# Feed-forward products as four column groups of the array, in a kernel of two attentions and a feed-forward block

## The chip, the cores and the metric

The kernel runs on one core of a Trainium2 chip. The metric is the device time of one execution in microseconds (us). The engines of the core are named as in the profile: PE is TensorE (matmuls), PEld its weight loads, DVE is VectorE, ACT is ScalarE, POOL is GpSimd, and SP issues most transfers.

## What is computed

The input x has shape (2, 256, 128, 128): batch, time, band, channel, all in fp32. Three blocks follow each other, each with a layer norm ahead of it and a residual sum behind it:

```
x = x + mha_over_time(ln(x))      # 4 heads of 32, causal over 256 times, for each band
x = x + mha_over_bands(ln(x))     # 4 heads of 32, |i - j| <= 16 over 128 bands, for each time
h = gelu(ln(x) @ w1.T + b1)       # 128 -> 512
x = x + (h @ w2.T + b2)           # 512 -> 128
```

The matrices of the attentions are 128 x 128 for query, key, value and output. A token has 128 channels, and there are 65536 tokens.

## The kernel before

The work is cut into groups of 512 tokens: 128 groups of attention over time (class OverTime), 128 over bands (OverBands), and 128 of feed-forward (FeedForward). First all time groups run. Then 16 runs follow; each has 8 band groups and after them 8 feed-forward groups over the same tokens. Changes from bands to feed-forward occur 16 times, back to bands 15 times.

The method run (from L1031) writes out the order of everything by hand, step by step. A step n holds pieces of several neighbouring groups: the scores or first hidden products of group n, the products that consume the softmax or the gelu of group n - 1 (weigh), the output projection of n - 2, projections of queries, keys and values of n + 1 or n + 2, and normalization of groups further on. Each engine runs its instructions in exactly this order, since every call goes through InOrder (L851), which pins it. That is why nearly all lines of the profile read L861: groups of instructions are told apart by the tile that they write.

The tiles of TensorE are these. xnT is the normalized input, channels on the partitions, 512 tokens. qp, kp (L568) and vp (L587) are the projections; sp the scores; rp the sums of the exponentials, by a product with ones; op the weighted values; yp (L627) the output projection. In feed-forward, hp (L808) is a hidden product, four a group, each with 512 tokens as moving columns; zp (L836) is the second product: for each of four blocks of 128 tokens it accumulates four products over the hidden index j, so sixteen products of 128 moving columns a group. All these tiles take turns in the 8 banks of PSUM. A product with fp32 operands appears in the trace as two MATMUL records and two weight loads.

An attention has a head in each band of 32 columns or rows of the array. Its scores use 32 rows of the array for a head (32*128 in the profile); rp and op use 32 columns for a head (128*32). Full products show as 128*128. For the projections, the helper product (L643) has both forms. With by_columns it issues four matmuls, each with 32 columns of the weights and 32 partitions of the output, all with the same moving operand; without, it issues one. run sets by_columns at L1058, once for each step: true where group n - 1 is an attention. The projections of steps behind a feed-forward group are therefore issued in full form: 66 qp and kp, 132 vp (33 groups) and 64 yp (16 groups), the few groups at the start of the program among them. hp and zp do not use the helper and are always in full form.

At a change from bands to feed-forward the step called turn first issues all four hp of the first feed-forward group, then rp, op and yp of the band groups that are still open. The next step has two hp, the zp of the first group, two hp, and the last yp of the bands. At a change back, the projections and scores of the first band groups stand between the last hp and zp. DVE normalizes, corrects the reciprocal of rp (writing rp, u, oT), adds residuals, and masks one head in four; ACT does exp, gelu and the copies out of PSUM; POOL masks and adds.

Of the kernel before, what the change touches and what calls it, by code (L numbers as in the profile page):

```python
# [19 lines left out]
P = 128  # L20
# [404 lines left out]
class Group:  # L425
# [117 lines left out]
    def weigh(self):  # L543
        pass
# [14 lines left out]
class Attention(Group):  # L559
# [8 lines left out]
    def queries_keys(self):  # L568
        path = self.path
        wf = path.k.wf[self.which]  # L570
        self.qp = path.bank([P, NT * P], "qp", self.place.get("qp", path.held.pop("qp", None)))
        product(path, self.qp, wf[:, 0:P], self.xnT)

        self.kp = path.bank([P, NT * P], "kp", self.place.get("kp"))
        product(path, self.kp, wf[:, P : 2 * P], self.xnT)
# [11 lines left out]
    def values(self):  # L587
        path = self.path
        wv = path.k.wf[self.which][:, 2 * P : 3 * P]
        self.vp = path.bank([P, NT, P], "vp", self.place.get("vp"))  # L590
        for i in range(NT):
            product(path, self.vp[:, i], self.xnT[:, i * P : (i + 1) * P], wv)
# [46 lines left out]
def rows_of(h):  # L639
    return slice(h * D, (h + 1) * D)  # L640


def product(path, out, weights, x):  # L643

    if not path.by_columns:
        path.tensor.matmul(out, weights, x, start=True, stop=True)
        return
    for c in range(P // D):
        path.tensor.matmul(out[rows_of(c)], weights[:, rows_of(c)], x, start=True, stop=True)


class OverTime(Attention):
# [75 lines left out]
def time_scores(old, new):  # L728


    if new is not None:
        new.first_tiles()
    if old is not None:
        old.second_tiles()
    for h, second, s in (
        (0, 1, 0), (1, 0, 0), (2, 0, 0), (3, 1, 0), (0, 1, 1), (3, 1, 1), (0, 0, 0), (3, 0, 0),
        (1, 0, 1), (2, 0, 1), (0, 0, 1), (3, 0, 1), (1, 1, 0), (2, 1, 0), (1, 1, 1), (2, 1, 1),
    ):
        if second and old is not None:
            old.second_scores(h, s)  # L740
        if not second and new is not None:
            new.first_scores(h, s)
# [57 lines left out]
class FeedForward(Group):  # L800
# [7 lines left out]
    def hidden(self, js):  # L808
        path = self.path
        for j in js:  # L810
            self.hp[j] = path.bank([P, NT * P], "hp")
            path.tensor.matmul(self.hp[j], path.k.w1f[:, j * P : (j + 1) * P], self.xnT, start=True, stop=True)

    def gelus(self, js):
        path = self.path
# [20 lines left out]
    def weigh(self):  # L836
        path, NI = self.path, self.path.k.NI
        self.zp = path.bank([P, NT, P], "zp")
        for i in range(NT):
            for j in range(NI):  # L840
                path.tensor.matmul(
                    self.zp[:, i], self.hT[:, j, i * P : (i + 1) * P], path.k.w2T[:, j, :],
                    start=(j == 0), stop=(j == NI - 1),
                )

# [20 lines left out]
class BoundedPath:  # L866
# [164 lines left out]
    def run(self, x, out):  # L1031
        groups = list(self.groups(x, out))

        def do(n, *names):
            if 0 <= n < len(groups):
                for name in names:
                    getattr(groups[n], name)()

        def at(n, kind):
            return 0 <= n < len(groups) and isinstance(groups[n], kind)  # L1040

        def do_at(n, kind, *names):
            if at(n, kind):
                do(n, *names)
# [8 lines left out]
        for n in range(-12, len(groups) + 2):  # L1053
            feeds = [at(n - 2 + i, FeedForward) for i in range(5)]
            bands = [at(n - 2 + i, OverBands) for i in range(5)]
            turn = feeds[2] and bands[1]
            old, new = (groups[i] if at(i, OverTime) else None for i in (n, n + 1))
            self.by_columns = at(n - 1, Attention)  # L1058
            if bands[2] and feeds[1]:
                self.scalar.preload_act_table_set(EXP_SET)  # L1060
            do_at(n + 4, FeedForward, "root")
            do(n, "first_half", "first_function", "first_mask")
            if old is not None or new is not None:
                time_scores(old, new)
                b = self.banks
                Attention.place = dict(rp=b["b0"], op=b["b3"], yp=b["a1"], qp=b["a2"], kp=b["b1"], vp=b["b2"])
            else:
                Attention.place = {}
            if old is not None:
                old.second_weights(old.late)  # L1070
            if new is not None:
                new.first_weights(new.early)
            if old is not None:
                old.second_weights(old.early)
                old.mask_second()
                old.add(0)
            if turn:
                do(n, "second_half", "second_function")
            do_at(n + 3, OverTime, "fetch")
            do_at(n + 2, (OverBands, FeedForward), "fetch")  # L1080

            for i in (2 * n + 12, 2 * n + 13) if n < -2 else (n + 10,) if n < 2 else ():
                if i >= NT:
                    do(i, "load")
            if n < -8 or n >= 0:
                do(n + 12, "load")
            if n >= 0:
                do_at(n + 5, OverTime, "statistics")
                for i in due[n]:
                    do(i, "statistics")  # L1090
            do_at(n + 3, (OverBands, FeedForward), "normalize", "turn")
            do_at(n + 4, OverTime, "normalize", "turn")
            if n < 0:
                do(n + 5, "statistics")
            do_at(n + 5, FeedForward, "statistics")
            if n == -4:
                self.fold_rest()
                self.warm()
            do(n - 1, "weigh")
            do(n - 1, "invert_exactly" if turn else "invert")  # L1100
            if new is not None:
                new.first_weights(new.late)
                new.mask_first()
            if old is not None:
                old.add(1)
            if bands[2] or turn or old is not None:
                do(n - 2, "output", "finish")
            do(n - 1, "divide")
            if not turn:
                do(n, "second_half", "second_function")  # L1110
            if n in run0:
                do(n, "bias")
            if not bands[2] and old is None:
                do_at(n, FeedForward, "bias")
                do_at(n + A, OverBands, "bias")
                if at(n - 1, FeedForward) and at(n - 2, OverBands):
                    do_at(n + A - 1, OverBands, "statistics", "root")
                if not turn:
                    do_at(n + A, OverBands, "statistics", "root")
            do_at(n + 2, OverTime, "queries_keys", "take_query", "take_key")  # L1120
            do_at(n + 1, OverBands, "queries_keys", "take_query", "take_key")
            do_at(n + 5, OverTime, "root_by_scalar", "refine")
            for i in due[n]:
                do(i, "root_by_scalar", "refine")
            do_at(n, OverTime, "bias")
            if not bands[2] and not turn and old is None:
                do(n - 2, "output", "finish")
            do_at(n + 2, OverTime, "values", "take_values")
            do_at(n + 1, OverBands, "values", "take_values")
            if old is not None or new is not None:  # L1130

                b = self.banks
                self.banks = dict(
                    a1=b["a1"], a2=b["a2"], b0=b["a0"], b3=b["a3"], a0=b["b0"], a3=b["b1"], b1=b["b3"], b2=b["b2"]
                )
# [69 lines left out]
```

## Time and profile before

| | |
|---|---|
| time, median of 3 runs | 2729.12 us (2726.89 to 2729.46) |
| span of the profiled run | 2727.3 us |
| granted clock of TensorE | 0.998 of full |
| busy DVE, ACT, POOL | 2280.3, 1846.0, 1861.1 us |
| records of MATMUL, of weight loads | 43538 each |
| the chain that ended last: PE, DVE | 83%, 13% |

The profile was taken on one execution. A line of groups gives the line, the engine, the operation, the tile written and the tiles read, the part of the array as rows*columns, the shape, the number of records, and behind the bar the busy time in us and the mean of one record in ns; behind the second bar is the idle time of the engine ahead of them. A line of the timeline gives the start in us, the length in us, and then the same names; x32 means that 32 records were merged. The ends of matmuls are modelled, and records of TensorE may overlap. In the chain of waits, the products zp and hp hold 17% and 14% of the span.

### The profile page before, as it was taken

To read this page: it belongs to the slowest core of one execution; us is meant where nothing else is said; L and a number is where in the kernel's file an instruction comes from. 1 tells how busy PE (TensorE), PEld (TensorE's weight loads), DVE (VectorE), ACT (ScalarE), POOL (GpSimd) and SP (SyncE) were. 2 spreads that over 40 slices of the span, in tenths; PEclk is the share of its full clock that TensorE was granted. 3 is DMA by queue.
4 is the path that set the end of the run, shared out by engine and by line. 5 is a ranking of instruction groups with operands and counts; after the bars stand their busy time and mean duration, and the time that the engine had idled before them with its cause. 6 is when DMAs were issued, how large, how long until landed. Compare 5 with 4: busy or idle time off the path is not lost.

```text
span 2727.3 us, 105790 instructions
## 1 busy us (share of the span) xinstructions
PE 2697.7 (99%) x43538; PEld 1884.5 (69%) x43538; DVE 2280.3 (84%) x6708; ACT 1846.0 (68%) x3620; POOL 1861.1 (68%) x2169
## 2 busy tenths in 40 slices
PE   7999999999999999999999999999999999999998
PEld 5666667767667667676676776766766767767666
DVE  7999999999999987968869779688697796886874
ACT  6888888888888874655745646556556466465563
POOL 3887888888788776666656666666576665665762
PEclk9999999999999999999999999999999999999999
DMA  5555555555555544444444444454453444534533
GB/s 147 146 149 142 146 151 141 152 147 142 145 153 143 136 108 120 116 117 126 111 119 127 106 120 118 116 129 106 121 130 102 122 120 110 135 108 115 132 91 79
DMA packets 471310, 343.84 MB, mean 126 GB/s; under 512 B 43296, under 2 KB 405152, under 8 KB 470816
## 3 DMA queue, kind: packets, MB, share of 16 engines
q1 hardware_dynamic: 469568, 335.92, 47.5%
q8 instruction: 344, 5.64, 0.9%
q10 hardware_dynamic: 1248, 1.05, 0.2%
q14 instruction: 150, 1.23, 0.2%
HBM read 169.03 MB, written 167.77 MB: 123 GB/s over the span
## 4 chain that ended last, share of the span: by engine, by line
PE 83%; DVE 13%; DMA 2%; issue 1%; SPq 0%; ACT 0%; DVEq 0%; ACTq 0%
PE zp L861 17%; PE hp L861 14%; PE sp L861 10%; PE op L861 8%; PE rp L861 7%; PE vp L861 7%; PE qp L861 6%; PE kp L861 6%; PE yp L861 6%; DVE xh L861 3%; DVE stats L861 2%; DVE z L861 2%; DVE u L861 2%; DVE rp L861 1%; DMA xnT<-turned 1%; DVE x L861 1%
## 5 line engine op out<-in xcount | busy, mean ns | idle before, releaser
L861 ACT ACTIVATE hT<-hp,b 128x512 f32<-128x512 f32 x512 | 347.8, 687 | 544.0 <-PE hp L861 533.1
L861 POOL TENSOR_SCALAR_AFFINE_SELECT pf<-pf 128x512 f32<-128x512 f32 x768 | 476.9, 635 | 268.8 <-ACT pf L861 242.5
L861 DVE TENSOR_SCALAR xh<-x,mv,rstd 128x160 f32<-128x160 f32 x1536 | 597.3, 432 | 14.2
L861 PEld LDWEIGHTS zp<-w2T_sb,hT 128*128 128x128 f32 x4096 | 476.3, 192 | 56.2 <-issue 54.0
L861 PE MATMUL zp<-w2T_sb,hT 128*128 128x128 f32 x4096 | 479.8, 275 | 0.1
L861 PE MATMUL hp<-xnT,w1f 128*128 128x512 f32 x1024 | 469.2, 596 | 0.0
L861 ACT ACTIVATE p<-sp 128x512 f32<-128x512 f32 (+1 forms) x1024 | 417.1, 501 | 17.3 <-PE sp L861 4.8
L861 POOL TENSOR_SCALAR_AFFINE_SELECT p<-p 128x1024 f32<-128x1024 f32 x256 | 280.1, 1094 | 191.8 <-ACT p L861 191.8
L861 PE MATMUL sp<-qT,kT 32*128 32x128 f32 (+1 forms) x8192 | 362.4, 310 | 3.2 <-DVE oT L861 1.9
L861 PEld LDWEIGHTS sp<-qT,kT 32*128 32x128 f32 x8192 | 310.1, 185 | 54.5 <-ACT kT L861 44.4
L861 PEld LDWEIGHTS vp<-wf,xnT 128*32 128x32 f32 (+1 forms) x7400 | 237.5, 113 | 153.3 <-issue 137.0
L861 POOL TENSOR_TENSOR p<-p,p 128x512 f32<-128x512 f32 x256 | 328.5, 1283 | 10.7
L861 DVE BATCH_NORM_STATS2 stats<-x 128x6 f32<-128x128 f32 x1536 | 327.0, 276 | 0.8 <-DMA x<-in_x 0.8
L861 ACT ACTIVATE pf<-sp 128x512 f32<-128x512 f32 x512 | 264.7, 603 | 60.8 <-PE sp L861 60.1
L861 PEld LDWEIGHTS hp<-xnT,w1f 128*128 128x128 f32 x1024 | 182.1, 190 | 174.7 <-issue 109.3
L861 DVE TENSOR_TENSOR res<-zp,res 128x512 f32<-128x512 f32 x128 | 87.5, 684 | 237.0 <-PE zp L861 237.0
L861 DVE STREAM_TRANSPOSE z<-xh 128x512 f32<-128x512 f32 x384 | 273.3, 712 | 13.2
L861 POOL TENSOR_SCALAR rstd<-mv 128x4 f32<-128x4 f32 x248 | 56.3, 227 | 319.6 <-DVE mv L861 318.5
L861 PE MATMUL vp<-wf,xnT 128*32 128x128 f32 (+1 forms) x7400 | 272.0, 273 | 0.0
L861 PE MATMUL yp<-wn,oT 128*32 128x128 f32 (+1 forms) x7808 | 271.2, 273 | 0.0
L861 POOL TENSOR_TENSOR rstd<-rstd,mhalf 128x4 f32<-128x4 f32 x248 | 256.6, 1035 | 20.7
L861 ACT ACTIVATE qT<-qp,bq 128x512 f32<-128x512 f32 x256 | 176.0, 687 | 137.5 <-PE qp L861 137.5
(92 smaller groups left out, 4215.9 us busy)
## 6 DMA issues: line engine op xcount, KB each, us to landing
turned<-z SPq DMA_DIRECT2D x1536, 64.0 KB, 1.9
xnT<-turned SPq DMA_DIRECT2D x384, 256.0 KB, 3.0
x<-in_x SPq DMA_DIRECT2D x128, 256.0 KB, 4.2
x<-res SPq DMA_DIRECT2D x256, 128.0 KB, 2.4
x<-x SPq DMA_DIRECT2D x128, 256.0 KB, 4.1
out<-res SPq DMA_DIRECT2D x256, 128.0 KB, 2.5
w1T_sb<-in_w1T ACTq DMA_DIRECT2D x1, 256.0 KB, 7.1
w2T_sb<-in_w2T ACTq DMA_DIRECT2D x1, 256.0 KB, 8.5
```

The source lines that it names most:

```text
L861: return self.tc.keep_in_program_order(emit(*args, **kwargs))
```

## The change

All products with full weights are issued in one form of the array. The helper loses its full form and takes the flags of accumulation; hp and zp are issued through it; the switch by_columns goes, so that the projections at the changes are in columns too. Each product becomes four matmuls of 32 weight columns that write 32 partitions each. The purpose is that the array stays in column groups from one product to the next, and leaves that form only for the scores. What is computed, the banks, and the order of products stay as they are.

```
-def product(path, out, weights, x):
-
-    if not path.by_columns:
-        path.tensor.matmul(out, weights, x, start=True, stop=True)
-        return
+def product(path, out, weights, x, start=True, stop=True):
     for c in range(P // D):
-        path.tensor.matmul(out[rows_of(c)], weights[:, rows_of(c)], x, start=True, stop=True)
+        path.tensor.matmul(out[rows_of(c)], weights[:, rows_of(c)], x, start=start, stop=stop)
...
-            path.tensor.matmul(self.hp[j], path.k.w1f[:, j * P : (j + 1) * P], self.xnT, start=True, stop=True)
+            product(path, self.hp[j], path.k.w1f[:, j * P : (j + 1) * P], self.xnT)
...
-                path.tensor.matmul(
-                    self.zp[:, i], self.hT[:, j, i * P : (i + 1) * P], path.k.w2T[:, j, :],
+                product(
+                    path, self.zp[:, i], self.hT[:, j, i * P : (i + 1) * P], path.k.w2T[:, j, :],
                     start=(j == 0), stop=(j == NI - 1),
                 )
...
-            self.by_columns = at(n - 1, Attention)
```

## The prediction

> **What bounds the kernel now.** I read the busy shares first, then the groups of TensorE, the windows of single steps, the waits of TensorE, and last its timeline at the steps that the diff touches. The shares say that one engine is full from end to end:
>
> ```profile
> PE 2697.7 (99%) x43538; PEld 1884.5 (69%) x43538; DVE 2280.3 (84%) x6708; ACT 1846.0 (68%) x3620; POOL 1861.1 (68%) x2169
> ```
>
> Of 2727.3 us TensorE (PE) lacks 30. Whole steps taken by windows say who is second. The first is one feed-forward step, the second one band step, from a product's start to the same product of the next step:
>
> ```profile
> 2043.17:2050.18 7.01, 7.01 (x42) 5.10 (x41) 3.92 (x15) 2.75 (x5) 3.74 (x6) 1.00 0.48 136
> 2088.59:2095.02 6.43, 6.43 (x160) 4.32 (x155) 6.29 (x19) 5.04 (x10) 4.95 (x9) 1.00 0.41 106
> ```
>
> The columns are length, then busy PE, PEld (weight loads), DVE, ACT, POOL. In the feed-forward step PE is full and the next, DVE, has 3.1 us free: what PE gains there is time gained. In the band step DVE works 6.29 of 6.43 us, so a gain of PE between bands could be lost to DVE. From 1000 us on one wait of PE recurs, once in each of the 16 runs, at the change from bands to feed-forward:
>
> ```profile
> PE rp L861 <- DVE u L861: 4.4, 16, 0.4
> ```
>
> Now the price of a product in either form. The groups mislead:
>
> ```profile
> L861 PE MATMUL zp<-w2T_sb,hT 128*128 128x128 f32 x4096 | 479.8, 275 | 0.1
> L861 PE MATMUL yp<-wn,oT 128*32 128x128 f32 x7680 | 254.3, 273 | 0.0
> ```
>
> A product is two records in full form, eight in columns (four groups, two passes). Busy by product is 479.8/2048 = 0.234 us for zp (full) and 254.3/960 = 0.265 for yp (columns): columns 13% dearer. But ends of matmuls are modelled and stretches overlap, so I take distances from start to start in the timeline. Feed-forward; band; the change to feed-forward; the change to bands:
>
> ```profile
> 2043.17 3.73 PE L861 MATMUL zp<-w2T_sb,hT 128*128 128x128 f32 x32
> 2046.74 3.60 PE L861 MATMUL hp<-xnT,w1f 128*128 128x512 f32 x8
> ...
> 2088.59 1.04 PE L861 MATMUL qp<-xnT,wf 128*32 128x512 f32 x8
> 2089.44 1.04 PE L861 MATMUL kp<-xnT,wf 128*32 128x512 f32 x8
> 2090.30 1.06 PE L861 MATMUL vp<-wf,xnT 128*32 128x128 f32 x32
> 2091.29 1.17 PE L861 MATMUL sp<-qT,kT 32*128 32x128 f32 x32
> 2092.39 1.06 PE L861 MATMUL rp<-pf,ones 128*32 128x512 f32 x8
> 2093.28 1.06 PE L861 MATMUL op<-pf,v 128*32 128x128 f32 x32
> 2094.15 1.06 PE L861 MATMUL yp<-wn,oT 128*32 128x128 f32 x32
> 2095.02 0.61 PE L861 MATMUL qp<-xnT,wf 128*32 128x512 f32 x4
> ...
> 2118.40 1.07 PE L861 MATMUL rp<-pf,ones 128*32 128x512 f32 x8 [0.26 <-DVE u L861]
> 2119.26 1.08 PE L861 MATMUL op<-pf,v 128*32 128x128 f32 x32
> 2120.13 1.08 PE L861 MATMUL yp<-wn,oT 128*32 128x128 f32 x32
> 2121.15 1.98 PE L861 MATMUL hp<-xnT,w1f 128*128 128x512 f32 x4
> 2122.97 0.27 PE L861 MATMUL zp<-w2T_sb,hT 128*128 128x128 f32 x1
> ...
> 2066.46 3.84 PE L861 MATMUL zp<-w2T_sb,hT 128*128 128x128 f32 x32
> 2070.14 1.02 PE L861 MATMUL qp<-xnT,wf 128*128 128x512 f32 x2
> ```
>
> Sixteen zp take 2046.74 - 2043.17 = 3.57 us, 0.2232 each. Four yp in columns take 2095.02 - 2094.15 = 0.873 us (to the nanosecond), 0.2183 each. Wide products cost 0.86 in both forms (kp 2090.30 - 2089.44; four hp take 3.44).
>
> **What the Trainium skill says.** "Perfetto Trace Analysis", section "Tensor Engine Instruction (MATMUL, LD_WEIGHTS)": the reported end of a matmul is an estimate from its size. The trace agrees: that zp "lasts" 3.73 us, and its successor starts after 3.57. "TensorEngine Tiling (Array Packing)", "Key Properties": a change of tiling mode drains the engine. The trace agrees with a cost: yp before an hp in full form takes 2121.15 - 2120.13 = 1.02 us instead of 0.87. "TensorE: Matmul & The Clock Gate", "Wait — 56ns, not 53.3ns?": starts never come closer than about 25 ns, and in one decoding mode a matmul costs the sequencer 62. The trace contradicts both as limits here: the band step's 152 records in 6.43 us are 42 ns each, and the four groups of a pass start 7 ns apart.
>
> **The change, part by part.**
> 1. zp in columns. 16 x (0.2232 - 0.2183) = 0.078 us by group; 128 groups: **10.1 us**. That accumulation over j costs nothing is taken from op of the time groups, which accumulates in columns; bounds 0 and 10.1.
> 2. hp in columns: 4 x (0.859 - 0.858), 128 times: **0.3**.
> 3. Scores to zp, 15 times (all runs but the last lead back to bands). Full zp takes 3.68 after sp, 3.57 after hp: 0.10 to enter full form. Scores to rp in columns cost 0.88 to 0.89 for a product of 0.86, so 0.03 remains; 15 x 0.08 = **1.2**.
> 4. First band group of a run: vp in full form, restarted after its wait for ACT, takes 1.09 us up to the scores; in columns, 0.99. 15 x 0.10 = **1.5**. kp's wait of 0.08 for ACT's qT stays: ACT follows qp at a fixed distance.
> 5. The second yp before feed-forward: 1.014 instead of 0.873, and the two hp behind it 1.82 instead of the usual 1.72. 16 x 0.24 = **3.9**.
> 6. The same pair one step earlier (yp, then hp, at 2113.46): 0.11 + 0.10 by run, worth 3.4, but **I count nothing**. Behind this hp stands rp, waiting for DVE's u. DVE runs without a wait from 2086.2, through 2118.4; PE would come 0.2 us sooner and wait 0.26 + 0.2. Bounds 0 and 3.4.
> 7. Four yp in full form between hp's: 0.89 against 0.87, 16 times: **0.3**.
>
> qp and kp in full form (0.86) gain nothing. No wait is added, only TensorE's instructions multiply: by 3 x (512 hp + 2048 zp + 66 qp and kp + 132 vp + 64 yp) = 8466 matmuls, from 21769 to 30235. The queues of the other engines keep their order. Sum 10.1 + 0.3 + 1.2 + 1.5 + 3.9 + 0.3 = 17.3; 2729.1 - 17.3 = **2711.8**, said as 2712.
>
> Does another engine catch the gain? After rp at 2118.4 DVE has no gap until past 2139. Its results that PE needs there (oT ready at 2127.1 for yp at 2128.26, closest) leave over 0.7 us; PE gains 0.4 by then. In plain feed-forward a gelu of 0.69 us ends some 0.9 us before zp needs it.
>
> **The rivals.**
> A. Only the changes of form gain: zp keeps 0.223 in columns, because accumulation or the long burst costs 5 ns a product. Then items 3 to 7: 2729.1 - 7.2 = 2722. For: no stretch before has more than 32 column products' matmuls of 128 columns in a row (op, yp); zp makes 64. Against: op and yp hold 109 ns a pass throughout.
> B. The issue of instructions becomes the limit and it is **slower**. From vp at 2083.87 to the qp at 2088.59 there are 136 records in 4.72 us, 34.7 ns each: the densest stretch that the trace proves. zp needs 128 records in 3.49 us, 27.3 each. Were 34.7 the ceiling, and a lead of 16 records built up during hp, zp would take 112 x 34.7 = 3.89 us, 0.32 more than now: 128 x 0.32 - 7.2 = +34, 2763. Against: the feed-forward step as a whole (160 records in 6.93 us, 43 each) is no denser than the band step (42), which never starves.
> C. The busy columns were right: zp +0.031 x 2048 = +63, hp from 469.2/512 = 0.916 to kp's 1.041, +64: 2856. The timeline speaks against it, since four yp do start 0.873 us before the next product.
> D. The gain at the turn (item 6) is kept as well, as DVE follows something of PE that I missed: 2708.
>
> **How the numbers follow.** Forecast (2709.5 to 2714) 0.66; A, with what lies between, 0.16; B 0.08, of which a little within 0.2%; C 0.01; D 0.06; elsewhere 0.03. The range 2708 to 2722 holds forecast, D and A up to its centre. Faster by over 0.2% means below 2723.7: forecast, D and most of A, 0.87; within 0.2%: 0.05; slower: 0.08.
>
> **What would show it.** In the profile after: sixteen zp from start to start 3.49 us (3.57 speaks for A, above for B); four hp 3.43; zp after scores about 3.52; yp before hp 0.87 and two hp 1.72 at both places; rp's wait for u grown from 4.4 us to about 8 (unchanged, with a shorter run, speaks for D); PE with some 60500 records. A new idle time of PE inside zp with "issue" as its end would make the prediction wrong, and so would a new wait of PE for DVE or ACT in feed-forward steps.

## The result, and the profile after

| kernel | median us | against the kernel before |
|---|---|---|
| before | 2729.21 (2726.89 to 2729.46) | |
| changed | 2709.97 (2708.88 to 2711.59) | 0.9932, 95% interval 0.9915 to 0.9949 |

The span of the profiled run fell from 2727.3 to 2709.9 us, by 17.4. Two repeats of the changed kernel, beside later experiments, gave 0.9943 (0.9929 to 0.9956) and 0.9941 (0.9927 to 0.9955), so the gain is 14 to 19 us by the times. Below, the first line is that of busy shares, the two after it are of the groups of PE, and the last is from the waits of PE from 1000 us on:

```profile
PE 2677.1 (99%) x60470; PEld 1831.5 (68%) x60470; DVE 2279.5 (84%) x6708; ACT 1845.1 (68%) x3620; POOL 1864.3 (69%) x2169
```

```profile
L859 PE MATMUL zp<-w2T_sb,hT 128*32 128x128 f32 x16384 | 475.8, 273 | 0.2 <-ACT hT L859 0.2
L859 PE MATMUL hp<-xnT,w1f 128*32 128x512 f32 x4096 | 474.6, 592 | 0.0
```

```profile
PE rp L859 <- DVE u L859: 7.6, 16, 0.6
```

PE issues 60470 records in place of 43538 and is busy 20.6 us less. Again the busy times of the groups say little: that of zp fell by 4.0 us and that of hp rose by 5.4. From start to start, in the timeline of the changed kernel (feed-forward, then a turn, then the change to bands), it reads otherwise:

```profile
2018.38 3.70 PE L859 MATMUL zp<-w2T_sb,hT 128*32 128x128 f32 x128
2021.88 3.64 PE L859 MATMUL hp<-xnT,w1f 128*32 128x512 f32 x32
2025.31 3.71 PE L859 MATMUL zp<-w2T_sb,hT 128*32 128x128 f32 x128
...
2102.15 1.06 PE L859 MATMUL yp<-wn,oT 128*32 128x128 f32 x32
2103.02 3.62 PE L859 MATMUL hp<-xnT,w1f 128*32 128x512 f32 x32
2107.09 1.07 PE L859 MATMUL rp<-pf,ones 128*32 128x512 f32 x8 [0.45 <-DVE u L859]
...
2108.81 1.08 PE L859 MATMUL yp<-wn,oT 128*32 128x128 f32 x32
2109.69 1.93 PE L859 MATMUL hp<-xnT,w1f 128*32 128x512 f32 x16
2111.40 0.32 PE L859 MATMUL zp<-w2T_sb,hT 128*32 128x128 f32 x4
```

Sixteen zp take 3.49 us (3.57 before), four hp 3.43 (3.44). The second yp ahead of hp takes 0.873 (1.014 before), the two hp behind it 1.72 (1.82). From the first yp to rp it is 4.94 to 4.95 us in both kernels, and there the wait for DVE has grown. One wait is new, of 0.2 us, once, by a zp for ACT's hT near the end of the program. The prediction named a new wait in feed-forward as a sign against it; this one is too small and too rare to matter.

A measure that leaves the first half out is the period of a run, from the yp ahead of one turn to that of the next. Its median is 108.72 us before and 107.75 after: 0.97 us a run, 15.5 us in 16 runs. The other 1.8 us of the span lie before the first turn (1026.03 us before, 1024.24 after), where both kernels do nearly the same. In the other kernels below, the first turn lies between 1023.0 and 1025.7 us, whatever their change; I count those 1.8 us as scatter.

### The profile page after: what moved, and what is told of

Read it like the earlier page. It is cut to its first block, busy times and chain, and to the rows that moved or that the text cites. A ratio compares the mean times of both kernels' runs of the same rounds, so it can differ in the third digit from the quotient of the medians.

```text
span 2709.9 us, 139654 instructions
## 1 busy us (share of the span) xinstructions
PE 2677.1 (99%) x60470; PEld 1831.5 (68%) x60470; DVE 2279.5 (84%) x6708; ACT 1845.1 (68%) x3620; POOL 1864.3 (69%) x2169
## 4 chain that ended last, share of the span: by engine, by line
PE 84%; DVE 12%; DMA 2%; issue 1%; SPq 0%; ACT 0%; DVEq 0%; ACTq 0%
PE zp L859 17%; PE hp L859 14%; PE sp L859 11%; PE op L859 8%; PE rp L859 7%; PE vp L859 7%; PE qp L859 7%; PE kp L859 7%; PE yp L859 6%; DVE xh L859 2%; DVE stats L859 2%; DMA xnT<-turned 2%; DVE z L859 2%; DVE u L859 2%; DVE rp L859 1%; DVE x L859 1%
## 5 line engine op out<-in xcount | busy, mean ns | idle before, releaser
L859 PEld LDWEIGHTS zp<-w2T_sb,hT 128*32 128x32 f32 x16384 | 459.3, 110 | 61.5 <-issue 37.2
L859 PE MATMUL zp<-w2T_sb,hT 128*32 128x128 f32 x16384 | 475.8, 273 | 0.2 <-ACT hT L859 0.2
L859 PE MATMUL hp<-xnT,w1f 128*32 128x512 f32 x4096 | 474.6, 592 | 0.0
L859 PEld LDWEIGHTS vp<-wf,xnT 128*32 128x32 f32 x8192 | 232.7, 110 | 157.3 <-issue 138.8
L859 PEld LDWEIGHTS hp<-xnT,w1f 128*32 128x32 f32 x4096 | 156.3, 110 | 190.0 <-issue 115.5
L859 PE MATMUL yp<-wn,oT 128*32 128x128 f32 x8192 | 271.8, 273 | 0.0
L859 PE MATMUL vp<-wf,xnT 128*32 128x128 f32 x8192 | 270.9, 273 | 0.0
L859 PE MATMUL qp<-xnT,wf 128*32 128x512 f32 x2048 | 267.2, 592 | 2.0 <-ACT p L859 2.0
```

What stands on the lines that cost most here:

```text
L859: return self.tc.keep_in_program_order(emit(*args, **kwargs))
```

## The experiments

The times were taken on three chips, and the kernel before was run beside each set: its median was 2726.06 us beside e1 to e4, 2724.93 beside e5 to e8, and 2726.26 beside e9 to e11. Ratios are against these. The expectations count from 2729, so I compare differences rather than times. I call a change from one form of the array to another a passage.

**The change taken apart.** Three kernels, e1 to e3, have one part of it each.

e1: zp alone in columns (hp keeps its single matmul, the projections keep by_columns; the helper can be told the form):

```
+    if not (path.by_columns if columns is None else columns):
+        path.tensor.matmul(out, weights, x, start=start, stop=stop)
...
-                path.tensor.matmul(
-                    self.zp[:, i], self.hT[:, j, i * P : (i + 1) * P], path.k.w2T[:, j, :],
-                    start=(j == 0), stop=(j == NI - 1),
+                product(
+                    path, self.zp[:, i], self.hT[:, j, i * P : (i + 1) * P], path.k.w2T[:, j, :],
+                    start=(j == 0), stop=(j == NI - 1), columns=True,
```

> Only zp in columns; hp and the projections at the changes as before. My theory (a product in columns is 5 ns cheaper at 128 moving columns, but every passage between full and column form costs TensorE time): sixteen zp still repeat 109 ns a pass, but each feed-forward step now has one passage into columns and one back. Back costs 0.24 us (yp to hp before the change: 0.14 and 0.10), into columns 0.1 to 0.2; less 0.08 gained: +0.25 to +0.36 a group, x 128 = +32 to +46 us, so 2761 to 2775 us. Rival (the form has no price of its own in a dense stream, and the gain at the changes had another cause): 2729 - 10 = 2719.

Measured: 2755.41 us, ratio 1.0100 (1.0083 to 1.0117): slower, by 29 us against the kernel before beside it, where I had expected 32 to 46. Its timeline in feed-forward:

```profile
2058.61 3.70 PE L861 MATMUL zp<-w2T_sb,hT 128*32 128x128 f32 x128
2062.24 3.70 PE L861 MATMUL hp<-xnT,w1f 128*128 128x512 f32 x8
2065.87 3.70 PE L861 MATMUL zp<-w2T_sb,hT 128*32 128x128 f32 x128
```

zp up to the next hp takes 3.63 in place of 3.49, and hp 3.63 in place of 3.43 or 3.44. A step has one passage into columns and one back, and they cost 0.14 + 0.20 = 0.34 us together, four times the 0.08 that zp gains. The rival, that the form has no price of passage, is out.

e2: the projections at the changes alone in columns:

```
-            self.by_columns = at(n - 1, Attention)
+            self.by_columns = True
```

> Only the projections at the changes in columns; hp and zp stay in full form. My theory: each change now has more passages. The yp between two hp goes out of full form and back (0.35 x 16 = +5.6 us), and the projections of the first two band groups are entered from hp or zp in full form (0.1 to 0.2, 2 x 15 times = +3 to +6); nothing in feed-forward is gained: 2738 to 2741 us. Rival (columns are cheaper by themselves): 2729 minus 1 to 3 us.

Measured: 2736.32 us, 1.0029 (1.0018 to 1.0041). Slower, by 8 to 10 us, at the lower end of the 9 to 12 expected. The yp in columns between full hp's takes 1.01 us (2023.57 to 2024.58) in place of 0.87 among column products, and each neighbour pays 0.09 to 0.10:

```profile
2021.76 1.88 PE L861 MATMUL hp<-xnT,w1f 128*128 128x512 f32 x4
2023.57 1.08 PE L861 MATMUL yp<-wn,oT 128*32 128x128 f32 x32
2024.58 1.98 PE L861 MATMUL hp<-xnT,w1f 128*128 128x512 f32 x4
2026.40 3.73 PE L861 MATMUL zp<-w2T_sb,hT 128*128 128x128 f32 x32
```

e3: hp and zp in columns, the projections as before (the edit of zp above, and the same for hp):

> hp and zp in columns; the projections at the changes in full form as before. My theory: the 10 us of zp are there, but full yp, qp, kp and vp now stand between column products: yp between two hp leaves and enters (0.35 x 16 = 5.6), and qp is entered from hp and from zp (0.24 x 30 = 7): 13 us above the changed kernel, 2723. In its trace the copy qT starts 1.06 us after the first record of a full qp, as before, against 1.16 in the changed kernel; so vp of the first band group should start about 0.1 us sooner after qp than there. Rival (passages are free): 2710.

Measured: 2723.37 us, 0.9987 (0.9979 to 0.9996). Its period is 108.55 us, 0.80 above the changed kernel's, which makes 12.8 us in 16 runs, where 13 were expected. That the time itself is the one expected is partly chance, since the kernel before was 3 us quicker beside it than the 2729 that I counted from. So the half that touches nearly all the work brings 3 us, the half at the changes costs 8 to 10, and both together bring 14 to 19: each half alone makes passages that the other takes away. The expectation for qT missed: it started 1.16 us after the first record of qp here too, since a full qp behind a column product begins with its passage (0.96 us to kp in place of 0.86). So e3 can't show how soon ACT follows a full product.

**Two groups in place of four**, for hp and zp (e4; all other products stay as in the changed kernel):

```
+def halves(path, out, weights, x, start=True, stop=True):
+    for c in range(2):
+        r = slice(c * P // 2, (c + 1) * P // 2)
+        path.tensor.matmul(out[r], weights[:, r], x, start=start, stop=stop)
```

> As the changed kernel, but hp and zp as two matmuls of 64 columns each in place of four of 32. If the 5 ns of a product come from the width of the weight load, the pass at 128 moving columns lies between 109.1 and 111.6 ns, at about 110, and each change pays passages between the 64 form and the 32 form: 2713 to 2725 us. If any split of the columns lets the loads run beside the matmuls, the pass is 109.1 as with four, and the time is 2710 plus the passages alone, 2713 to 2720. If two groups hide less than four and than one, zp is slower than 3.57 us and the time above 2729.

Measured: 2722.36 us, 0.9983 (0.9976 to 0.9991). In feed-forward two groups of 64 columns run as fast as four of 32, 3.49 us for zp and 3.43 for hp:

```profile
2026.12 3.66 PE L865 MATMUL zp<-w2T_sb,hT 128*64 128x128 f32 x64
2029.61 2.74 PE L865 MATMUL hp<-xnT,w1f 128*64 128x512 f32 x12
```

So the 5 ns of a product don't follow the width of a group; both splits tried remove them, as the second alternative had it. Whether loads that run beside matmuls are the reason is not shown. That alternative's time, at most 2720, was too low: the passages between groups of 64 and of 32 cost more than I allowed. The period is 108.48 us, 0.72 above the changed kernel's. Within feed-forward zp and hp cost the same in both; the difference lies at the changes, where for example yp in 32s ahead of hp in 64s takes 0.99 to 1.01 us in place of 0.87.

**The turn.** The prediction counted nothing for the first yp and hp of a turn, since rp waits there for DVE's u. What ties them is a bank of PSUM. In each step of band attention weigh reserves (holds) two banks, for yp and for the qp of the next group. At a turn no qp follows. With four hp, two held banks, rp and op the step uses all eight, and rp falls on the bank of the rp before, which u frees. First attempt (e6): hold the second bank only where a band group's qp follows.

```
-        path.held = dict(yp=path.turn_of_bank(), qp=path.turn_of_bank())
+        path.held = dict(yp=path.turn_of_bank())
+        if path.hold_query:
+            path.held["qp"] = path.turn_of_bank()
...
+            self.hold_query = bands[3]
```

The changed kernel beside it as a measure (e5):

> The changed kernel once more, beside the three next on one chip: 2710 us, ratio to the kernel before 0.993.

Measured: 2711.13 us, 0.9943 (0.9929 to 0.9956). With the edit (e6):

> The changed kernel, with a bank of PSUM held for the next qp only in steps where a band group's qp will follow. It computes the same. rp at the turn then takes a bank that was free long before, in place of the one that DVE's u releases, and the first qp of a run no longer takes a bank that vp takes right after it. My theory (item 6: at the turn TensorE is held by DVE through this bank alone): the wait of rp for u, 7.6 us in 16 waits, goes, and so does vp's wait for qT, some 0.18 us x 15 = 2.7 us: 2700 us. Rival (DVE is the bound there as such, and the wait only moves to op, yp or hp): 2706 to 2710, with a new wait of PE for DVE in the same step.

Measured: 2711.79 us, 0.9947 (0.9933 to 0.9961): nothing gained, where I had expected 2700, but for another reason than the rival's. The wait left the turn and came back larger elsewhere:

```profile
PE rp L861 <- DVE oT L861: 13.5, 16, 1.0
```

I had overlooked the step ahead of the turn. There too no qp follows; without its hold, that step's rp falls on the bank of the last op. In the changed kernel oT is done with that op only 0.75 us after this rp starts, so here rp comes 0.9 us later. At the turn itself, from yp to rp, the trace shows 4.31 us in place of 4.95; but since PE lost 0.9 us just ahead of it, this alone does not show that DVE's lag is harmless there. The same edit on the kernel before (e7):

> The kernel before with the same edit of the banks. Its wait of rp for u is 4.4 us and vp's wait for qT 0.08 us x 15 = 1.3: 2723.5 us. With the wait gone, the passage from yp to hp ahead of it (item 6, 0.21 us x 16 = 3.4) counts in this kernel and not in the changed one. So the distance between this kernel and e6 should be 17.4 + 3.4 + 1.4, about 22 us, against 17 to 19 without the edit. Rival (item 6 is not lost by the wait but never existed): the distance stays at 17 to 19.

Measured: 2732.83 us, 1.0029 (1.0018 to 1.0040), with the same 13.5 us of new wait, and 4.65 us from yp to rp. The distance of the two periods is 109.095 - 107.811 = 1.28 us, 0.97 without the edit. The forecast time failed: I had expected 6 us less than the kernel before, and it is 8 us more. The distance, 20.5 us in 16 runs, is near the 22 forecast.

Half of the edit, the leftover bank dropped behind the turn (e8):

```
+            if feeds[1]:
+                self.held.pop("qp", None)
```

> The changed kernel, with only the leftover bank for qp dropped behind a turn: vp's wait for qT in the first band group goes, rp's wait for u stays. My theory: 0.18 us x 15 = 2.7 us less than the changed kernel, 2707. Rival (ACT is the bound of that stretch, so sp waits for kT in place of vp for qT): 2709 to 2710.

Measured: 2709.03 us against 2711.13 on the same chip. The single times of the two overlap (2705.51 to 2711.10 and 2707.48 to 2711.76), so they don't decide between theory and rival; the trace does. The period is 107.58, 0.17 less than the changed kernel's. vp starts 1.72 us after qp in place of 1.89, and the scores follow 0.17 us sooner. This wait was a clash of banks, and not a bound of ACT.

Then the hold dropped in the turn step alone, in the changed kernel (e9) and in the kernel before (e10), with the changed kernel once more beside them (e11):

```
+        if not path.at_turn:
+            path.held["qp"] = path.turn_of_bank()
...
+            self.at_turn = turn
```

> The changed kernel, with no bank held for a qp in the turn step alone (the step before keeps its hold, so its rp does not fall on the bank of the last op). By the trace of e6 the stretch from yp to rp at the turn is 4.31 us when nothing holds rp, against 4.95 in the changed kernel; op then comes 0.2 us behind the end of u, yp 0.5 behind oT. My theory: 0.64 us at each of 16 turns, and vp's wait in 15 first band groups (e8: 0.17 us each): the period of a run falls from 107.75 to about 106.95 us, and the time to 2697. Rival (DVE's lag shows up at the next product, op for u or yp for oT): 107.4 and 2704 to 2709.

> The kernel before with the edit of e9. If the passages between forms at the turn are hidden by the wait alone, they count here: yp to rp 4.65 us (e7) in place of 4.95, and the vp wait goes: period 108.72 to 108.23, time 2717 to 2719, and the distance to e9 is 1.28 us a run, 20.5 us, against 15.5 without the edit. Rival (the distance is the same with and without the wait): 0.97 us a run.

> The changed kernel beside e9 and e10 on one chip, as the measure for both: 2710 us, period of a run 107.75 us.

Measured: e9 2698.75 us, 0.9898 (0.9883 to 0.9913), period 106.92; e10 2718.53 us, 0.9971 (0.9960 to 0.9983), period 108.20; e11 2711.69 us, 0.9941 (0.9927 to 0.9955), period 107.75. e9 is 13 us shorter than the changed kernel beside it. The turn in e9, with the u of DVE, and in e10:

```profile
2093.82 1.06 PE L861 MATMUL yp<-wn,oT 128*32 128x128 f32 x32
2094.69 3.62 PE L861 MATMUL hp<-xnT,w1f 128*32 128x512 f32 x32
2098.12 1.04 PE L861 MATMUL rp<-pf,ones 128*32 128x512 f32 x8
...
2097.93 0.69 DVE L861 SCALAR_TENSOR_TENSOR u<-rp,r 128x512 f32<-128x512 f32 x1
```

```profile
2107.74 1.06 PE L863 MATMUL yp<-wn,oT 128*32 128x128 f32 x32
2108.72 3.70 PE L863 MATMUL hp<-xnT,w1f 128*128 128x512 f32 x8
2112.35 1.07 PE L863 MATMUL rp<-pf,ones 128*32 128x512 f32 x8
```

No idle stands ahead of either rp. Column products take 2098.12 - 2093.82 = 4.30 us, the mixed forms 2112.35 - 2107.74 = 4.61. The 0.31 is the price of the two passages up to the start of rp, paid in e10 and hidden by the wait in the kernel before. The distance e10 to e9 is 1.28 us a run, as forecast, against 0.97.

## Why the prediction was right, point by point

The forecast was 2712, a gain of 17.3 us, and the medians are 2709.97, 2711.13 and 2711.69. That the last two lie so near is partly luck: the kernel before ran 3 to 4 us quicker beside them, so the gains are 19.2, 13.8 and 14.6. Item by item, from start to start, by medians:

| item | predicted us | trace after |
|---|---|---|
| 1 zp in columns | 10.1 | 0.078 x 128 = 10.0 |
| 2 hp in columns | 0.3 | 3.436 to 3.433: 0.4 |
| 3 scores to zp | 1.2 | zp there 3.675 to 3.518, less item 1: 1.2 |
| 4 first band group of a run | 1.5 | qp to scores 2.887 to 2.904: -0.3 |
| 5 second yp and its two hp | 3.9 | 0.14 + 0.10, 16 times: 3.9 |
| 6 first yp, hp at the turn | 0 | yp to rp 4.95, unchanged: 0 |
| 7 yp between hp's | 0.3 | 0.3 |
| sum | 17.3 | 15.5 |

The sum agrees with the 15.5 of the periods. The 17.3 met the profile's 17.4 partly by luck: item 4 was wrong, and the scatter of the first half filled its place. One slip in the working changes nothing: the 7.2 us of rival A are items 2 to 7; items 3 to 7 come to 6.9.

**Item 4 failed at the sentence that kp's wait stays at 0.08 since "ACT follows qp at a fixed distance".** The distance is not the same for both forms. The kernel before had it in its own trace: qT starts 1.06 us after the first record of a full qp at a change, and 1.11 after one in columns behind a yp. At this place in the changed kernel it is 1.15 by the median; why the last 0.04 are added is open. Start of qp, vp and scores before and after, and of ACT's copy qT:

```profile
2062.47 1.02 PE L861 MATMUL qp<-xnT,wf 128*128 128x512 f32 x2
...
2064.27 1.16 PE L861 MATMUL vp<-wf,xnT 128*128 128x128 f32 x8
2065.36 1.17 PE L861 MATMUL sp<-qT,kT 32*128 32x128 f32 x32
```

```profile
2051.30 1.07 PE L859 MATMUL qp<-xnT,wf 128*32 128x512 f32 x8
...
2053.20 1.08 PE L859 MATMUL vp<-wf,xnT 128*32 128x128 f32 x32
2054.21 1.17 PE L859 MATMUL sp<-qT,kT 32*128 32x128 f32 x32
```

```profile
2063.53 0.69 ACT L861 ACTIVATE qT<-qp,bq 128x512 f32<-128x512 f32 x1 [0.17 <-PE qp L861]
```

```profile
2052.46 0.69 ACT L859 ACTIVATE qT<-qp,bq 128x512 f32<-128x512 f32 x1 [0.21 <-PE qp L859]
```

In these lines qT starts 1.06 us after a full qp and 1.16 after one in columns. vp, which waits for qT, starts 1.90 after qp in place of 1.80, and what it saves up to the scores (1.09 to 1.01) is gone. The 1.09 was misread as well: with the wait removed, the stretch from qp to the scores is 2.70 us in full form (e7, e10) and 2.71 to 2.73 in columns (e6, e8, e9). So there was nothing to win, with or without that wait.

**Item 6 was right in kind, and its upper bound too low.** e9 and e10 show 0.31 us at a turn, 5.0 us in all, where the prediction had 3.4 as the upper end: it left out the passage from the full hp to rp in columns. The wait did grow, 4.4 to 7.6 us in the profile's account, some 8 being forecast. Those 3.2 us are less than the 5.0 that the passages cost; the idle time of PE is counted from modelled ends of matmuls, so it can't measure them. But the reason given, that DVE lags, is only half of it. DVE does lag; what made PE wait for it was one bank. In e9 the lag is the same (u ends 4.80 us after that yp starts, 2098.62 - 2093.82, as in the changed kernel, 1999.19 - 1994.39), and rp starts 0.5 us before u ends.

**The rivals.** A (zp keeps its price in columns) falls with the 3.49 us. B (issue) falls with it: 128 records of zp start in 3.49 us, 27 ns each. C (busy columns) forecast 2856. D (the gain at the turn is kept) forecast 2708; the times alone would not exclude it; that the stretch from yp to rp at the turn stayed at 4.95 us does.

## What to carry to other kernels

Price a product from the start of one group to the start of the next: busy time by product had the sign wrong here (columns 13% dearer, where they are 2% cheaper). Choose a form of the array for the whole stream of products: here one passage costs more than the form gains in a whole group; changing half of the products made the kernel slower (e1, e2) or left it nearly level (e3). Where an engine waits for a lagging one, look for the buffer that ties them before calling the lagging engine the bound, and follow a change of buffers one step back as well as at the place it is meant for.

## What the runs showed of the hardware

In fp32 with 128 moving columns a product costs 223.2 ns as one matmul (3.571 us for sixteen zp), 218.3 as two of 64 columns or four of 32 (3.493 us); with 512 moving columns 859 against 858. Why one matmul is 5 ns dearer is not settled; e4 shows that it doesn't follow the width of the groups. A passage from four column groups to full form costs 0.22 to 0.24 us: 0.11 to 0.14 at the end of the column product and 0.10 at the start of the full one. The way back costs 0.12: 0.09 at the end of the full product (e2) and 0.03 at the start of the column one (e10, rp up to op: 0.883 in place of 0.858 us). In e1 both together cost 0.34. Between groups of 64 and of 32 columns there is a passage too: in e4 yp ahead of hp takes 0.99 to 1.01 us in place of 0.87, and the two hp behind it 1.77 in place of 1.72. The copy qT by ACT starts 1.11 to 1.15 us after the first record of a qp in four columns, and 1.06 after a full one that no passage precedes.
